# Last turn's last layer in halves, bias rows spread by a product, three x loads first, 25 early sums and three late batches

## The chip, the cores and the metric

The kernel runs on one core of a Trainium2 chip. The metric is the device time of one execution in microseconds (us); lower is better. A run is given as the median of several executions. Beside them one execution was recorded by the hardware profiler; its engines are called PE (matrix products; PEld are its weight loads), DVE (vector), ACT (activation functions and copies), POOL (the general engine) and SP (here it only issues transfers).

## The reference

32 graphs of 512 nodes with 128 features go through four layers, each added to its input after a normalization. `adj` is a 0/1 matrix, symmetric, with ones on its diagonal. Cut to what matters:

```python
# x: (32, 512, 128), adj: (32, 512, 512)
h = relu(layernorm(x))                       # layer 0: masked attention
q, k, v = relu(h @ Wq.T + bq), relu(h @ Wk.T + bk), relu(h @ Wv.T + bv)
x = x + softmax(where(adj, q @ k.T, -inf)) @ v

h = relu(layernorm(x))                       # layer 1: weights made by an LSTM
dyn = conv1d(h[:, -128:, :], conv_w) + conv_b
lw = lstm(dyn)                               # 128 steps, one after the other
x = x + sigmoid(A_norm @ h @ lw)             # A_norm = D^-1/2 (adj + I) D^-1/2

nodes = relu(layernorm(x))                   # layer 2: four layers, each reads earlier ones
for i in range(4):                           # of 128, 128, 256, 384 inputs
    src, dst, own = nodes @ ws + bs, nodes @ wd + bd, nodes @ wn + bn
    new = tanh(concat(l2norm(adj, 2) @ src, own, l2norm(adj, 1).T @ dst) @ wu + bu)
x = x + new

h = relu(layernorm(x))                       # layer 3
y = adj.T @ (h @ W.T) + bias
x = x + prelu(y, a)
```

## The kernel before, in words

**A plan makes the order.** The program is written as a list of operations. Each has an engine (or two to choose from), an estimated duration, a rank, and what it reads and writes. `Plan.run` simulates the engines with these durations and gives out operations in the order in which they could start, the lower rank first. The order found is the order of each engine's queue on the chip, and each queue runs strictly in it. Some constants steer the simulation: `HOLD`, the time by which an operation of other work may still overlap an awaited step of the LSTM; `AHEAD`, `KEEP` and `FETCH`, a model of how many PE instructions have been fetched; `LEAD`, taken off the rank of the operations of the last turn's end.

**The stages.** `pass_1` treats every batch: load x, normalize, transpose, keys, values, the last 128 rows of the attention (`f_pk`, `f_pql`, `f_pv`, `f_sl`, `f_pol`), and the convolution (`f_pd`), whose result goes into `seq`. `fold(i)` multiplies layer 2's weights into two matrices per input, with weights loaded in pass 1 at the positions in `FOLD_AT`. The LSTM then runs 128 steps for all batches together (`f_z` on PE, tanh on ACT, the cell on DVE, a transpose into `seq` on DVE, L1349). Between its steps, `pass_2` does the other 384 rows of the attention (`f_pq`, `f_s`, `f_po`). Of 32 batches the first 24 (`EARLY`) also form layer 1's sums there (`f_pg`) and store them; two (`FIRST`) are kept in memory for the first turns after the LSTM; two (`NEXT`) follow them; the last four (`LATE`) get a rank behind these. Then `rest` does layers 1 to 3, one batch per turn, 32 turns, with neighbouring turns interleaved on PE.

**The start.** Parameters are loaded beside x on ACT's queue by `load_beside`: the attention's weights, the column biases, and row `R_V` of the biases, spread to all 128 partitions by the transfer. Then the table of exp is loaded. The row of the convolution's bias is loaded in the same spread manner on SP's queue (`w_crow`). Ranks of SP put x of the first batch first, then each batch's x and last adjacency columns `f_al` in turn. `warm_up` products on a tile of zeros keep PE busy until data are there: 20 at the start.

**The end.** In the last turn (number 31) each of layer 2's four layers is: `f_py` (a product per 128 nodes with folded weights, onto a bias that ACT or DVE wrote into the bank), split into two parts (`f_y`, L1501 and L1502), eight products with the adjacency into `f_pa` (L1538), a scaling on DVE (L1654), the product with the node's own weights (L1658), and tanh (L1662). After the last one `f_n4T` transposes the result, DVE adds it to x (L1679), `relu_first` normalizes all four tiles of x, with one power on POOL (L1091), and splits them (L1525 on ACT, L1527 on DVE). Products with the adjacency go into two half banks (L1693), are copied to `f_g`, and are multiplied by W (`f_p`, L1706). Then come three steps on each half: DVE adds the positive part (L1709), ACT takes the negative part (L1713), DVE adds it scaled (L1714), and it is stored (L1719). Turns 29 and 30 put off L1713, L1714 and the store until the last turn's split is made; their L1709 comes at once. 16 warm-up products stand in the last turn behind `f_n4T`. At the very end every engine loads a flag that says whether the inputs have the assumed form (L1753), after the stores have been issued, and branches past a general version of the program.

Of the kernel before, what the change touches and what calls it, by code (L numbers as in the profile page):

```python
# [9 lines left out]
AF = mybir.ActivationFunctionType  # L10
# [3 lines left out]
P = 128  # L14
# [507 lines left out]
class Plan:  # L522
# [15 lines left out]
    HOLD = 0.15  # L538
    AHEAD = 264
    FETCH = 4.8  # L540
    KEEP = 32
# [71 lines left out]
    def run(self, tc, queues):  # L613
# [15 lines left out]
        for o in ops:  # L629
            if o.rank >= self.last:  # L630
                k, sub = divmod(o.rank - self.last, 10)
                if sub == 2:
                    apart.add(o)
                soon = self.soon if k < 2 and sub < 2 else 0.0
                first = self.lead if sub == 4 else 0.0
                o.rank = self.last - soon + 12 * k - 9 * max(0, k - 28) + 200.0 - first - (min(behind[o], 60) if sub == 5 else behind[o] + (70 if sub == 2 else 0.0))
# [157 lines left out]
def symmetric(ctx, tc, x, adj, weights, cols, rows, lstm_b, prelu_a, out, fail):  # L794
# [19 lines left out]
    LATE = 4  # L814
    FIRST = [B - LATE - 2 + k for k in range(2)]
    EARLY = range(24)
    NEXT = [len(EARLY), len(EARLY) + 1]
    FOLD_AT = (2, 3, 4, 5)
# [4 lines left out]
    FIRST_GAPS = (2.0, 2.8, 3.0, 3.5)  # L823
    LEAD = 0.0
    Q_AT = 3
    MOVED = range(2, B - 2)
    TURN = 32
    T_STEP = 0.22
    SOON = 9_950.0
    LANDED = 3.3  # L830
# [44 lines left out]
    def t_act(n):  # L875
        return 0.17 + n * 0.0006
# [81 lines left out]
    def load_beside(dst, src, c, gap):  # L958
        return ACT(HEAD, 0.45, lambda: nc.scalar.dma_start(dst, src), [], [c], gap=gap)

    w_att, w_cols = plan.fixed(w), plan.fixed(colb)
    load_beside(w[:, :W_CONV, :], weights[:, :W_CONV, :], w_att, 3.5)
    load_beside(colb, cols, w_cols, 3.0)
    load_beside(brow[:, BR_V, :], rows[R_V].partition_broadcast(P), (biases, BR_V), 3.0)
    ACT(HEAD, 1.5, lambda: nc.scalar.activation(table, neg_half[:, 0, 0:1], AF.Exp))
    w_conv = load(HEAD + 12, 192, w[:, W_CONV:W_IH, :], weights[:, W_CONV:W_IH, :])
    w_crow = load(HEAD + 12, 64, conv_row, rows[R_CONV].partition_broadcast(P))
# [18 lines left out]
    for k in range(20):  # L986
        warm_up(HEAD, 0.43 if k < 8 else 0.216, f"f_warm_{k}")

# [3 lines left out]
    def fill(rank, dst, src, r, c, after):  # L992

        def mark():
            if not c.marked:
                nc.tensor.matmul(c.t, marks[:, :P], marks[:, : c.size], start=True, stop=True)

        def act():
            mark()
            nc.scalar.copy(dst(), src)  # L1000

        def dve():
            mark()
            nc.vector.tensor_copy(dst(), src)
        return plan.op({"ACT": (t_act(c.size), act), "DVE": (t_dve(c.size), dve)}, rank, r, [c], after)
# [158 lines left out]
    def pass_1(b, pos):  # L1164
        R = 10_000 + pos * 10
        xc = new("x", (P, NT, P), f"f_x_{b}")
        n = 2 if pos == 0 else NT
        for at in range(0, NT, n):
            DMA(R, 64 * n, lambda at=at: nc.sync.dma_start(xc.t[:, at : at + n, :], x[b].rearrange("(t p) d -> p t d", p=P)[:, at : at + n, :]), [],
                [(xc, t) for t in range(at, at + n)] if pos == 0 else [xc], gap=FIRST_GAPS[pos] if pos < len(FIRST_GAPS) else 3.5)  # L1170
# [11 lines left out]
        if pos == 0:  # L1182
# [32 lines left out]
        fill(R, lambda: pv.t, bias(BR_V), [(biases, BR_V)], pv, [turned])  # L1215
# [298 lines left out]
    def relu_first(rank, xc, name):  # L1514

        mv = ln_stats(rank, xc, range(NT), name)
        rs = new("rs", (P, NT), f"f_rs_{name}")
        ln_rstd(rank, mv, 0, NT, (lambda: rs.t[:, :], rs), True)
        y = new("xn", (P, NT, P), f"f_yr_{name}")
        parts = new("y", (P, NT, 2, P), f"f_xp_{name}", FR)  # L1520
        for t in range(NT):
            DVE(rank, t_dve(P), lambda t=t: nc.vector.tensor_scalar(y.t[:, t, :], xc.t[:, t, :], mv.t[:, t, 0:1], 0.0, OP.subtract, OP.max),
                [(xc, t), (mv, t)], [(y, t)])
        for t in range(NT):
            ACT(rank, t_act(P) + 0.13, lambda t=t: nc.scalar.activation(parts.t[:, t, 0, :], y.t[:, t, :], AF.Relu, scale=rs.t[:, t : t + 1]),  # L1525
                [(y, t), rs], [(parts, (0, t))])
            DVE(rank, t_dve(P), lambda t=t: nc.vector.scalar_tensor_tensor(  # L1527
                parts.t[:, t, 1, :], y.t[:, t, :], rs.t[:, t : t + 1], f32(parts.t[:, t, 0, :]), OP.mult, OP.subtract),
                [(y, t), rs, (parts, (0, t))], [(parts, (1, t))])
        for finish in put_off:  # L1530
            finish(parts.parts[0, NT - 1][0], parts.parts[1, NT - 1][0])
        return parts
# [19 lines left out]
    def state_of(b, lw):  # L1552

        return nc.sync.dma_start(lw.t.rearrange("t (j f) -> t j f", f=TURN), dh.t.rearrange("(j b) t f -> b t j f", b=B)[b])

    def rest(b, turn, lw_after):
# [83 lines left out]
        for i, nch in enumerate(L2_CHUNKS):  # L1640
            py = bank(f"f_py_{b}_{i}", (P, NT, P), filled=True)
# [24 lines left out]
        if moved:  # L1666
            n4, _ = by_transfer(R, lambda: nodes[4].t, nodes[4], "gs", f"d{b}")
            p4, p4_t = n4, lambda: n4.t
        else:
            p4 = bank(f"f_n4T_{b}", (P, NT, P))  # L1670
            p4_t = lambda: flat(p4.t)

            def back():
                turn_tiles(p4.t, lambda t: nodes[4].t[:, bass.ts(t, P)])
            end4 = PE(R, 4 * T_TR, back, [nodes[4]], [p4])
        if turn == B - 1:
            for k in range(2 * BUFS["mm"]):
                warm_up(R - 4, 0.216, f"f_warm_{k}_{b}", [end4])
        DVE(R, t_dve(N), lambda: nc.vector.scalar_tensor_tensor(flat(xc.t), p4_t(), 0.5, flat(xc.t), OP.add, OP.add),  # L1679
            [p4], [xc])  # L1680
# [7 lines left out]
        for at in range(0, NT, n) if n < NT else ():  # L1688
            cols = slice(at * P, (at + n) * P)
            p3a = bank(f"f_pg3_{b}_{at}", (P, n * P), whole=False)  # L1690
            for k in range(2):
                for j in range(NT):
                    agg3 = PE(R, t_r(n * P), lambda p3a=p3a, cols=cols, k=k, j=j: nc.tensor.matmul(  # L1693
                        p3a.t, hp.t[:, j, k, :], ar.t[:, j, cols], start=(k == 0 and j == 0), stop=(k == 1 and j == NT - 1)),
                        [(hp, (k, j)), ar], [p3a], count=2)
            evict(R, n * P, lambda cols=cols: g3.t[:, cols], lambda p3a=p3a: p3a.t, [p3a], [(g3, at)])
        neg = new("xn", (P, NT, P), f"f_neg_{b}")

        for at in range(0, NT, n):
# [4 lines left out]
            def fc_mm(at=at, p3=p3):  # L1704
# [4 lines left out]
            DVE(R, t_dve(n * P), lambda p3=p3, part=part: nc.vector.scalar_tensor_tensor(  # L1709
                flat(xc.t[:, part, :]), flat(p3.t), 0.0, flat(xc.t[:, part, :]), OP.max, OP.add), [p3], mine)  # L1710

            def finish(turned=(), split=(), at=at, p3=p3, part=part, mine=mine):
                ACT(R, t_act(n * P), lambda: nc.scalar.activation(neg.t[:, part, :], p3.t, AF.Relu, scale=-1.0), [p3], [(neg, at)], after=turned)  # L1713
# [7 lines left out]
            if turn in (B - 3, B - 2):  # L1721
                put_off.append(finish)
            else:
                stored = finish()
            if turn == B - 1:
                late.append(stored)
# [6 lines left out]
    def counted():  # L1733
# [21 lines left out]
        PE(R + 4, 0.1, read, [], [], after=[said] + late)  # L1755
# [105 lines left out]
```

## Time and profile before

| | |
|---|---|
| median of 3 runs | 1277.38 us (1276.59 to 1277.43) |
| the profiled execution | 1275.34 us |
| its span, first to last instruction | 1273.4 us |
| busy: PE, DVE, ACT, POOL | 1255.8 (99%), 985.9 (77%), 837.8 (66%), 400.7 us (31%) |
| weight loads PEld | 970.9 us (76%) |
| moved by transfers | 232.02 MB, mean 182 GB/s |

The span is 1.94 us shorter than the profiled execution's time, and that execution is 2.04 us shorter than the median. A busy PE is not PE at its peak: the ends of products are modelled, so the time from one start to the next says more than the busy share. In the chain of waits a line is: start in us, length in us, what ran; each piece was released by the one above it.

### The profile page before, as it was taken

Reading aid. Unit: us, or ns where it says so; the run is one execution under the profiler, and the core shown is the slowest. Engines: PE = TensorE matmul, PEld = TensorE weight load, DVE = VectorE, ACT = ScalarE, POOL = GpSimd, SP = SyncE. Lnnn points to the kernel's source line nnn. Section 1 sums busy time; section 2 is a strip of 40 time slices with the busy share of each in tenths; the row PEclk is TensorE's granted clock in tenths of the full one; section 3 lists DMA queues with packets and bytes.
Section 4 is the critical chain, followed back from the end, with each engine's and each line's share of the span. In section 5 each row is a group of like instructions: output and inputs, shape, how many; then the busy total and the mean of one; then the engine's idle time right before and its main releaser. Section 6 shows DMA issues by size and latency. Waiting matters only on the chain.

```text
span 1273.4 us, 33089 instructions
## 1 busy us (share of the span) xinstructions
PE 1255.8 (99%) x12074; PEld 970.9 (76%) x12075; DVE 985.9 (77%) x3275; ACT 837.8 (66%) x2102; POOL 400.7 (31%) x734
## 2 busy tenths in 40 slices
PE   9999999999999999999999999999999999999997
PEld 7988876666666767777778787787787877877775
DVE  7899869989899889775677677676776776787755
ACT  4667677778777667774576676666766766675433
POOL 3556533324233135331223233232242232332001
PEclk9999999999999999999999999999999999999999
DMA  8888887778986797876476677777777777482211
GB/s 270 255 274 277 275 270 233 213 226 272 277 259 214 213 251 210 174 175 160 83 178 156 155 173 160 153 174 152 175 154 151 175 157 153 89 174 59 50 33 37
DMA packets 313052, 232.02 MB, mean 182 GB/s; under 512 B 151601, under 2 KB 258481, under 8 KB 312881
## 3 DMA queue, kind: packets, MB, share of 16 engines
q1 hardware_dynamic: 295280, 212.65, 61.5%
q0 software_dynamic: 16896, 16.78, 8.5%
q8 instruction: 97, 1.59, 0.5%
q14 instruction: 75, 0.61, 0.2%
q10 hardware_dynamic: 704, 0.40, 0.1%
HBM read 135.73 MB, written 62.58 MB: 156 GB/s over the span
## 4 chain that ended last, share of the span: by engine, by line
PE 86%; DVE 6%; POOL 2%; ACT 2%; DMA 2%; issue 1%; SPq 0%; ACTq 0%; DVEq 0%
PE f_pa L1538 18%; PE f_py L1647 15%; PE f_pa L1658 15%; PE f_pg L1538 8%; PE f_po L1415 5%; PE f_z L1303 4%; PE f_s L1409 4%; PE f_pol L1251 2%; PE f_pk L1177 2%; PE f_p L1706 2%; PE f_sl L1241 2%; PE f_pv L1219 2%; PE f_pl L1612 2%; PE f_pd L1276 2%; PE f_pq L1399 1%; DVE f_e L1413 1%
## 5 line engine op out<-in xcount | busy, mean ns | idle before, releaser
L1538 PE MATMUL f_pa<-f_ar,f_y 128*128 128x512 f32 x1024 | 298.0, 428 | 0.2 <-ACT f_y L1501 0.2
L1538 PEld LDWEIGHTS f_pa<-f_ar,f_y 128*128 128x128 f32 x1024 | 189.3, 188 | 73.1 <-issue 38.7
L1647 PE MATMUL f_py<-f_wf,f_n 128*128 128x128 f32 x1280 | 173.7, 275 | 0.0
L1647 PEld LDWEIGHTS f_py<-f_wf,f_n 128*128 128x128 f32 x1280 | 165.0, 191 | 10.1 <-issue 2.9
L1662 ACT ACTIVATE f_n<-f_pa,f_bcol 128x512 f32<-128x512 f32 x128 | 88.3, 690 | 101.9 <-PE f_pa L1658 99.0
L1658 PE MATMUL f_pa<-f_n,f_wf 128*128 128x512 f32 x320 | 152.7, 593 | 0.1
L1456 ACT ACTIVATE f_ar<-f_a 128x512 fp32r<-128x512 f32 x224 | 138.7, 622 | 4.1 <-PE f_pg L1538 2.4
L1463 POOL DMA_DIRECT2D f_das<-f_ar x32 | 27.1, 846 | 360.2 <-ACT f_ar L1456 338.1
L1501 ACT CAST f_y<-f_py 128x512 fp32r<-128x512 f32 x128 | 75.3, 589 | 72.1 <-PE f_py L1647 65.5
L1502 DVE TENSOR_TENSOR f_y<-f_py,f_y 128x512 fp32r<-128x512 f32 x128 | 87.7, 687 | 34.9 <-ACT f_y L1501 33.4
L1654 DVE TENSOR_TENSOR f_pa<-f_pa,f_inv 128x512 f32<-128x512 f32 x128 | 86.9, 694 | 28.0 <-PE f_pa L1538 27.9
L1415 PE MATMUL f_po<-f_v,f_e 128*32 128x129 f32 x3072 | 108.0, 273 | 0.4 <-DVE f_e L1413 0.2
L1415 PEld LDWEIGHTS f_po<-f_v,f_e 128*32 128x32 f32 x3072 | 90.9, 110 | 21.1 <-issue 16.6
L1658 PEld LDWEIGHTS f_pa<-f_n,f_wf 128*128 128x128 f32 x320 | 57.9, 190 | 47.0 <-issue 42.6
L1409 PE MATMUL f_s<-f_q,f_k 128*32 128x384 f32 x928 | 92.0, 486 | 0.2 <-issue 0.2
L1303 PE MATMUL f_z<-f_w,f_seq 128*32 128x128 f32 x2040 | 83.4, 276 | 5.2 <-DVE f_seq L1349 2.3
L1303 PEld LDWEIGHTS f_z<-f_w,f_seq 128*32 128x32 f32 x2040 | 53.0, 109 | 45.1 <-ACT f_e L1412 10.0
L1132 DVE COPY f_hl_d<-f_n 128x1024 uint16<-128x1024 uint16 x27 | 18.7, 694 | 88.0 <-ACT f_n L1662 88.0
L1472 DVE SCALAR_TENSOR_TENSOR f_aT<-f_a,f_aT 128x1024 bf16<-128x1024 f32 (+1 forms) x68 | 76.3, 1152 | 0.5 <-DMA f_aT<-f_das 0.5
L1647 PE MATMUL f_py<-f_wf,f_T_c 128*128 128x128 f32 x448 | 72.8, 275 | 0.0
L1538 PE MATMUL f_pg<-f_ar,f_xp_d 128*128 128x512 f32 x248 | 71.9, 413 | 0.0
L1538 PE MATMUL f_pg<-f_ar,f_xp_c 128*128 128x512 f32 x256 | 68.4, 407 | 0.6 <-ACT f_xp_c L1509 0.4
(213 smaller groups left out, 2755.1 us busy)
## 6 DMA issues: line engine op xcount, KB each, us to landing
f_a<-in_adj_dram SPq DMA_DIRECT2D x112, 256.0 KB
f_a<-in_adj_dram SPq DMA_DIRECT2D x28, 1024.0 KB
f_das<-f_ar POOLq DMA_DIRECT2D x32, 512.0 KB, 4.8
f_dkq<-f_kh SPq DMA_DIRECT2D x29, 448.0 KB
f_al<-in_adj_dram SPq DMA_DIRECT2D x32, 256.0 KB
f_inv<-f_ddi SPq DMA_DIRECT2D x32, 256.0 KB
f_x<-in_x_dram SPq DMA_DIRECT2D x31, 256.0 KB
out_dram<-f_x SPq DMA_DIRECT2D x31, 256.0 KB
```

The source lines that it names most:

```text
L1303: nc.tensor.matmul(z.t[part, k, :, :], h, w[:, m : m + 4, part], start=False, stop=True, skip_group_check=True)
L1409: PE(R, t_mm(NR), lambda s=s, j=j: quarters(lambda p: nc.tensor.matmul(s.t[p], keys_of()[:, j * P + p.start : j * P + p.stop], q_of(), sta ...
L1415: PE(R, t_mm(P), lambda e=e, t=t, j=j: quarters(lambda p: nc.tensor.matmul(po.t[p, t, :], e.t[:, t * P + p.start : t * P + p.stop], v.t[:, ...
L1456: ACT(rank, 0.62, lambda t=t: nc.scalar.activation(ar.t[:, t, :], a.t[:, t, :], AF.Square, accum_out=deg.t[:, t : t + 1]), [(a, t)], [(ar, ...
L1472: nc.vector.scalar_tensor_tensor(flat(aT.t[:, n * k : n * (k + 1), :]), flat(a.t[:, n * k : n * (k + 1), :]), 1.0, flat(aT.t[:, n * k : n ...
L1501: ACT(rank, t_act(N), lambda: nc.scalar.copy(parts.t[:, :, 0, :], src.t), [src], [(parts, 0)])
L1502: DVE(rank, t_dve(N), lambda: nc.vector.tensor_sub(parts.t[:, :, 1, :], src.t, f32(parts.t[:, :, 0, :])), [src, (parts, 0)], [(parts, 1)])
L1538: nc.tensor.matmul(pg.t, parts.t[:, j, k, :], ar.t[:, j, :], start=(k == 0 and j == 0), stop=(k == 1 and j == NT - 1))
L1647: nc.tensor.matmul(py.t[:, j, :], nodes[n].t[:, bass.ts(j, P)], wf[:, W_F[i] + c, 0, :], start=False, stop=(c == nch - 1), skip_group_chec ...
L1654: before = DVE(R, t_dve(N), lambda pa=pa: nc.vector.tensor_mul(pa.t, pa.t, inv_row.t), [inv_row], [pa])
L1658: nc.tensor.matmul(pa.t, wf[:, W_F[i] + c, 1, :], nodes[n].t, start=False, stop=(c == nch - 1), skip_group_check=True)
L1662: ACT(R, 0.57, lambda pa=pa, n=n, i=i: nc.scalar.activation(n.t, pa.t, AF.Tanh, bias=bcol[:, i : i + 1]), [pa], [n])
```

## The change

It does the following; parts that only rename are left out.

- The last turn's fourth layer (`BY_HALVES = (3,)`) is written by `layer_by_halves`: banks, splits, products and tanh over 256 columns at a time. `update_by_halves` transposes and adds each half, and `relu_first` has statistics and power for each half.
- In turns 29 and 30 L1709 is put off too; in turn 30 it waits for the last turn's split. L1713 is now ordered behind L1709.
- The last turn's warm-up products are 4 behind the transpose and 3 behind the last product with the adjacency, instead of 16. At the start they are 17 instead of 20.
- The flag is loaded after the copies to `f_g` instead of after the stores, and with a lower rank (R + 3 gets 60 taken off).
- At the start, two bias rows come in one transfer to one partition; a product with ones spreads them, and ACT copies them out. The load order on ACT's queue is column biases, table of exp, weights, rows. SP issues x of three batches before all else. The first batch's fill of `f_pv` is on ACT alone.
- `EARLY` 24 to 25, `LATE` 4 to 3 (so `FIRST` is 27, 28 and `NEXT` 25, 26), `FOLD_AT` one position later, and constants of the plan.

```diff
-    HOLD = 0.15
+    HOLD = 0.18
...
-    FETCH = 4.8
-    KEEP = 32
+    FETCH = 4.5
+    KEEP = 48
...
-                first = self.lead if sub == 4 else 0.0
+                first = self.lead if sub == 4 else 60.0 if sub == 3 else 0.0
...
-    LATE = 4
+    LATE = 3
...
-    EARLY = range(24)
+    EARLY = range(25)
...
-    FOLD_AT = (2, 3, 4, 5)
+    FOLD_AT = (3, 4, 5, 6)
...
-    FIRST_GAPS = (2.0, 2.8, 3.0, 3.5)
-    LEAD = 0.0
+    FIRST_GAPS = (2.0, 3.5, 4.0, 4.0)
+    LEAD = 3.0
...
-    LANDED = 3.3
+    LANDED = 2.8
...
-    load_beside(w[:, :W_CONV, :], weights[:, :W_CONV, :], w_att, 3.5)
     load_beside(colb, cols, w_cols, 3.0)
-    load_beside(brow[:, BR_V, :], rows[R_V].partition_broadcast(P), (biases, BR_V), 3.0)
     ACT(HEAD, 1.5, lambda: nc.scalar.activation(table, neg_half[:, 0, 0:1], AF.Exp))
-    w_conv = load(HEAD + 12, 192, w[:, W_CONV:W_IH, :], weights[:, W_CONV:W_IH, :])
-    w_crow = load(HEAD + 12, 64, conv_row, rows[R_CONV].partition_broadcast(P))
+    load_beside(w[:, :W_CONV, :], weights[:, :W_CONV, :], w_att, 3.0)
+    two_rows = flat(seq[:, : 2 * P // B, :])
+    nc.vector.memset(two_rows, 0.0)
+    w_rows = plan.fixed(two_rows)
+    load_beside(two_rows[0:1], rows[R_V : R_CONV + 1].rearrange("(o r) f -> o (r f)", o=1), w_rows, 2.5)
+    w_conv = load(HEAD + 22, 192, w[:, W_CONV:W_IH, :], weights[:, W_CONV:W_IH, :])
+    w_crow = plan.fixed(conv_row)
...
-    for k in range(20):
+    for k in range(17):
         warm_up(HEAD, 0.43 if k < 8 else 0.216, f"f_warm_{k}")
+
+    spread = bank("f_spread", (P, 2, P), whole=False)
+    PE(HEAD, t_mm(2 * P), lambda: nc.tensor.matmul(flat(spread.t), ones, two_rows, start=True, stop=True), [w_rows], [spread])
+    ACT(HEAD, t_act(P), lambda: nc.scalar.copy(brow[:, BR_V, :], spread.t[:, 0, :]), [spread], [(biases, BR_V)])
+    ACT(HEAD + 11, t_act(P), lambda: nc.scalar.copy(conv_row, spread.t[:, 1, :]), [spread], [w_crow])
...
-            DMA(R, 64 * n, lambda at=at: nc.sync.dma_start(xc.t[:, at : at + n, :], x[b].rearrange("(t p) d -> p t d", p=P)[:, at : at + n, :]), [],
+            DMA(R if pos > 2 else HEAD + pos, 64 * n, lambda at=at: nc.sync.dma_start(xc.t[:, at : at + n, :], x[b].rearrange("(t p) d -> p t d", p=P)[:, at : at + n, :]), [],
...
+    def layer_by_halves(R, b, i, nodes, ar, inv_row, before):
...
+        n = new(f"n{i + 1}" if i < 3 else "gs", (P, N), f"f_n{i + 1}_{b}")
+        nodes.append(n)
+        for at in range(0, NT, HALF):
+            cols = slice(at * P, (at + HALF) * P)
+            pa = bank(f"f_pa_{b}_{i}_{at}", (P, HALF * P), whole=False)
+            for k in range(2):
+                for half in range(0, NT, HALF):
+                    def quarter(pa=pa, cols=cols, k=k, half=half):
+                        for j in range(half, half + HALF):
+                            nc.tensor.matmul(pa.t, parts.t[:, j, k, :], ar.t[:, j, cols], start=(k == 0 and j == 0),
+                                             stop=(k == 1 and j == NT - 1))
+                    PE(R, HALF * t_r(HALF * P), quarter, [(parts, (k, half)), ar], [pa], count=2 * HALF)
+            before = DVE(R, t_dve(HALF * P), lambda pa=pa, cols=cols: nc.vector.tensor_mul(pa.t, pa.t, inv_row.t[:, cols]), [inv_row], [pa])
...
+            PE(R, nch * t_mm(HALF * P), own, [nodes[m] for m in CHUNKS[i]], [pa])
+            ACT(R, t_act(HALF * P) + 0.1, lambda pa=pa, cols=cols: nc.scalar.activation(n.t[:, cols], pa.t, AF.Tanh, bias=bcol[:, i : i + 1]),
+                [pa], [(n, at)])
...
-            for k in range(2 * BUFS["mm"]):
+            for k in range(4 if two else 7):
                 warm_up(R - 4, 0.216, f"f_warm_{k}_{b}", [end4])
...
+            for k in range(3 if at else 0):
+                warm_up(R - 4, 0.216, f"f_warm_{k}_{at}_{b}", [agg3])
...
+                up = DVE(R, t_dve(n * P), lambda: nc.vector.scalar_tensor_tensor(
+                    flat(xc.t[:, part, :]), flat(p3.t), 0.0, flat(xc.t[:, part, :]), OP.max, OP.add), [p3], mine, after=split if turn in WAITING else ())
...
-        PE(R + 4, 0.1, read, [], [], after=[said] + late)
+        PE(R + 3, 0.1, read, [], [], after=[said] + late)
```

## Prediction

> **What bounds the kernel now.** I read the page first, then the chain of waits, then busy time by stretch.
>
> ```profile
> PE 1255.8 (99%) x12074; PEld 970.9 (76%) x12075; DVE 985.9 (77%) x3275; ACT 837.8 (66%) x2102; POOL 400.7 (31%) x734
> PEclk9999999999999999999999999999999999999999
> L1303 PE MATMUL f_z<-f_w,f_seq 128*32 128x128 f32 x2040 | 83.4, 276 | 5.2 <-DVE f_seq L1349 2.3
> ```
>
> PE is the bound nearly everywhere; the change removes no matrix product but warm-ups. So only PE's idle time can be won: at the start, between LSTM steps, at the end. The chain at the start:
>
> ```profile
> 0.74 3.25 DMA f_w<-in_weights_dram
> 4.00 0.34 SPq L955
> 4.39 6.28 DMA f_x<-in_x_dram
> 10.70 0.48 DVE f_st_a L1081 x2
> 11.18 0.39 DVE f_kh L1180
> 11.71 1.14 PE f_sl L1241 x8
> ```
>
> SP issues the third batch's x only at 4.39; it lands at 10.67. DVE, in order, stands before its statistics, and behind them stands the first batch's key copy (L1180), for which PE waits until 11.71. The chain at the end:
>
> ```profile
> 1250.07 2.58 PE f_pa L1658 x6
> ...
> 1253.57 0.90 PE f_p L1706 x8
> ...
> 1254.57 0.70 DVE f_x L1709
> ...
> 1255.92 0.75 DVE f_x L1714
> 1256.67 0.61 DVE f_x L1679
> ...
> 1258.76 0.59 PE f_warm L984 x2
> 1259.35 0.89 PE f_p L1706 x8
> 1260.24 0.86 PE f_warm L984 x4
> ...
> 1263.45 1.09 PE f_warm L984 x5
> ```
>
> The last turn's result is ready at 1252.64, but its update (L1679) starts at 1256.6: its transposes stand behind other turns' products, and DVE behind turn 28's L1709 and L1714. Later PE runs warm-ups while inputs are there.
>
> ```profile
> L1753 PEldq TENSOR_LOAD <-fail x1: 488/488/488, 1265.9 to 1265.9; - x1
> L1753 SPq TENSOR_LOAD <-fail x1: 485/485/485, 1266.8 to 1266.8; - x1
> 1267.00:1268.00 1.00, 0.00 (x0) 0.00 (x0) 0.00 (x0) 0.00 (x0) 0.00 (x0) 1.00 0.68 177
> 1268.00:1269.00 1.00, 0.00 (x0) 0.00 (x0) 0.00 (x0) 0.00 (x0) 0.00 (x0) 0.54 0.40 106
> ```
>
> The flag is loaded behind the stores; nothing computes from 1266.83 to 1273.4. The last two lines (stretch, length, five engines, PE clock, transfers) show the clock falling.
>
> **The end: -1.9 us.** Halving adds no PE work: 8 products of 512 columns take 1.85 us, and 128x256 products run at 0.118 (10 in 1.18 us). It adds fixed cost: a 256-column DVE step is 0.42-0.43 us against 0.69, so three split steps cost 0.45 more; on ACT about 0.4; two POOL powers of about 0.69 (the first batch's pair: 1.38) against 1.07 add 0.3, on a POOL queue that holds nothing else after 1259 but its flag load. In return half 0 runs 1.3 us ahead (half of 2.58), and half 1 has less behind it: tanh 0.45 for 0.69, transposes 0.22 for 0.44, update 0.42 for 0.69, two statistics 0.43 for 0.87, power 0.7 for 1.07, two ACT splits instead of four (1.28): about 2 us less latency.
>
> Two floors say how much can show. PE after 1252.64: products of turns 28 to 30 (two f_pg halves 1.86, one f_pg of 1.85, three f_p at 0.89, transposes and flag sum 0.5) and the last turn's own 16 (1.87) are 8.8 us, to 1261.4, where before they ended at 1263.45: -2.0. DVE is busy 10.55 of the 12.37 us from 1254.5 to 1266.87, so without idle it ends 1.8 earlier, 3.0 if half 0's 1.2 us move into the idle DVE of 1250-1254 (1.98 of 4 us busy), less the 0.45. Putting turn 30's L1709 (0.69) behind the split lets L1527 start at 1260.3 instead of 1260.96; it then lies in DVE's wait of 1.1 us before the last f_p. Its cover is that wait; if DVE is not idle there, it costs 0.69. L1713 behind L1709 is nothing new: ACT already waited 1.7 us for it. Warm-ups were 3.0 us of the chain above; the seven left cost at most 7x0.216 = 1.5. I take -1.9, the lower end of both floors; bounds -3.0, and +0.5 if the held banks of turns 29 and 30 (two of eight) and the small banks of the halves make them wait for one another.
>
> The clock: by the row it is full to about 1268.1 (0.54 is 0.5 and 0.08 us of full), 1.8 us after the last product (1265.92+0.38). The Trainium skill (TensorE: Matmul & The Clock Gate, Part 1: The HAM clock gate) says that a window of 3.4 us without work halves it; that speaks against cutting warm-ups. If it fell, 16 f_pg and 8 f_p would take 2.8 us more. Neither row nor rule gives that: without 9 warm-ups the longest hole is the copy to f_g, under 1 us. I count 0.
>
> **The flag: -0.4 us.** Its load leaves the path on SP (0.485 us) and ACT (0.48). PE, with the lower rank, may load it ahead of the second half's f_p: +0.49 in the worst case; DVE and ACT load it in their wait for f_p (1.1 and 1.7 us). What remains is larger: SP's load ends at 1267.3, its next instruction comes at 1271.8. From the trace alone an earlier load might move all of this forward. The Trainium skill (Runtime: NRT & Kernel Launch, Instruction fetch mechanics) says that fetch runs ahead only in sequence and that a taken branch to a page not held waits for its transfer. Then the 4.5 us start at the branch, still behind the stores; by the rule -0.5, by the other reading up to -1.5 (how much earlier PE loads it). I follow the rule; bounds -0.5 and +0.5.
>
> **The start: -1.2 us.** PE's products from 7.24 to 14.02 are 4.1 us (f_xt, f_pk, f_pql, f_pv, f_sl, f_xt, f_wT at 0.44, 0.86, 0.22, 0.89, 0.89, 0.44, 0.33), so 2.7 us are idle; from 14.02 it is full. Issuing x of the third batch before 2.5 instead of 4.39 takes away DVE's 1.17 us wait and PE's 0.9 us hole: -0.9. SP's f_al slips by some 0.5 us; its first user (L1246) is at 13.58. The two spread rows (64 KB each; 0.34 us of SP's issue, 0.48 of ACT's) go, for one row transfer of 1 KB on ACT. The convolution weights slip a batch on SP; their user starts at 21.45. FOLD_AT moves 0.33 us of transposes out of a hole: later work, same sum. ACT's queue: the weights go behind the table load (1.28) and its activation (0.2), so are issued at about 2.7 instead of 0.74; with the same 3.25 us they land at 6.0, before f_pk at 8.30. Without them beside it x of the first batch may land earlier (192 KB at 267 GB/s: 0.7 us), and 17 warm-ups end 0.65 earlier; the spread product (two passes of 256 columns, 0.43) takes most of that back: -0.3. Its danger: it is in PE's queue ahead of the first transposes; rows issued at 3.2 land at about 6.4, warm-ups end at 6.5. If rows come later, all of PE waits, one for one. ACT has two copies (0.37 each) and the fill (0.59) more, in its idle 8.53-10.11. Bounds -2.7 and +0.7.
>
> **The LSTM's stage: -0.9 us.** 187.9 to 493.0 is 127 steps of 2.40 us. A stretch such as 445-465 holds 212 f_po, 72 f_s, 16 f_pq, 132 f_z and 8 f_pg, at their spacing (0.0275, 0.081, 0.081, 0.027, 0.23) 18.3 of 20 us; so over the stage some 20 us of PE are lulls and changes of tile form. The 25th early batch brings one f_pg (2.04 with its changes) into the stage and takes 1.85 out of PE-bound time: -1.85 if a lull takes it, +0.2 if not; I take half. It also brings DVE about 3.5 us (L1101, L1510, L1479, half an L915) where DVE is busy 273.1 of 308.2, and ACT's squares 4x0.62; 256 KB more stored and fetched, and 1 MB of adjacency again later, beside PE-bound turns at 150-175 GB/s, where earlier stretches carried 280. LATE changes order: at 493 only 168 f_po, under two batches, were left anyway: 0. HOLD, KEEP, FETCH, LANDED change when filler is let in; no row shows it. Bounds: -3 (a seventh of the lulls) and +3.8 (0.03 x 127), value 0, the nearest row being that PE waits only 2.3 us for L1349 in all.
>
> **Sum.** -1.9 - 0.4 - 1.2 - 0.9 = -4.4. The profiled execution, 1275.34 us (span 1273.4 and 1.94 around it), would become 1270.9. It lies 2.04 below the median of the runs; the same change on the median gives 1273.0.
>
> **Rivals.** *More from the stage.* Filler constants and the early batch win 4 us of lulls: 1277.4-3.5-4 = 1269.9. For it: 20 us are there, and 465-485 holds a POOL chain of 6 us. Against: DVE at 89%. *Gains don't show.* PE at the start is held by the spread product (0), the end gives 0.9 because turn 30's own chain (f_g at 1258.3, f_p at 1259.2) ends last: 1276.5. For it: turn 30 was on the chain at 1259.35. Or it doesn't do what it says: the plan, not ranks, sets where half 0 stands, and it may queue right before half 1. *Slower.* HOLD 0.18 lets filler overlap each awaited step by 0.03 us more; on two engines that is 0.06x127 = 7.6 us later LSTM end. Where PE fills this, it costs nothing; where filler waits for data it is lost: 1277.4-3.5+7.6 = 1281.5. It decides from about 0.03 us per step (2.43 us), unless less work is left behind the LSTM. Against: filler remained at 493.
>
> **How the numbers follow.** The likeliest case has 0.55 (own range 1270.8 to 1274.8), more from the stage 0.16, gains don't show 0.18, slower 0.11. A measurement can tell 0.2%, 2.55 us, from no change; so faster 0.71, same 0.18, slower 0.11. The range goes down to 1267.5 (most of the first rival, with the start's bound) and up to 1278.0, beyond which only the slower case lies.
>
> **What would show it.** Right: DVE's first wait for f_x after 5 us gone; PE from about 13 us full; the last f_pg by 1262 on this clock, i.e. 2 us closer behind L1658; TENSOR_LOAD on SP before the last store; still 4 to 5 us from branch to SP's next instruction; L1349 from first to last within 305 +-3 us. Wrong: a PE hole before f_xt, clock under 1.00 before the last f_p, or an LSTM span changed by more than 4 us.

## The result and the profile after

| | before | after |
|---|---|---|
| median of 6 runs each | 1277.41 us (1276.59 to 1279.67) | 1272.21 us (1270.56 to 1273.86) |
| ratio, 95% interval | | 0.9963 [0.9953, 0.9974] |
| profiled execution, its span | 1275.34, 1273.4 us | 1272.32, 1270.4 us |

The kernel became faster by 4.7 us (interval 3.3 to 6.0); the forecast was 1273.0. The two profiled executions differ by 3.0 us only, since that of before lay 2.07 us below its median and that of after 0.11 above. So the traces can be asked where 3.0 us went, and not more.

Five marks cut the span (us; starts, except where an end is named). They are read in every kernel below.

| mark | before | after | stretch before it changed by |
|---|---|---|---|
| first product `f_z` of the LSTM | 185.14 | 184.11 | -1.0 |
| first transpose of a step (L1349; after: L1361) | 187.9 | 188.2 | +1.3 |
| last such transpose | 493.0 | 498.2 | +5.0 |
| end of the last own product (L1658; after: L1609) | 1252.64 | 1253.62 | -4.3 |
| end of the last DVE step | 1266.83 | 1265.56 | -2.25 |
| end of the span | 1273.4 | 1270.4 | -1.7 |

**The page of after**, the three lines that were shown of before:

```profile
PE 1251.3 (98%) x12078; PEld 970.2 (76%) x12078; DVE 974.8 (77%) x3267; ACT 835.6 (66%) x2126; POOL 389.6 (31%) x737
PEclk9999999999999999999999999999999999999999
...
L1315 PE MATMUL f_z<-f_w,f_seq 128*32 128x128 f32 x2040 | 83.2, 276 | 7.3 <-DVE f_seq L1361 5.0
```

PE is still the bound at a full clock. In the third line, the idle time of PE before an LSTM product grew from 5.2 to 7.3 us, with 5.0 of it waiting for the step's transpose (before: 2.3).

**The start**, in the chain of waits of after (start us, length us, what):

```profile
1.23 3.34 DMA f_x<-in_x_dram
...
8.28 1.01 POOL f_rs_a L1103
9.30 0.22 POOL f_rs_a L1102
...
9.59 1.08 POOL f_rs_a L1103
...
11.47 0.70 DVE f_kh L915
...
12.21 1.13 PE f_pk L1189 x2
```

No transfer of x stands in the chain after 4.57 us; before, one of 6.28 us ended at 10.67. From 12.21 the chain is PE without a break to 20 us (before: from 14.02). What is late next is POOL: its powers lead to the second batch's key copy, for which PE still waits 0.9 us.

**The end**, the same view:

```profile
1251.04 2.59 PE f_pa L1609 x12
1253.62 0.89 PE f_p L1791 x8
1254.52 0.44 PE f_n4T L1624 x4
1254.95 2.81 PE f_pg L1555 x12
...
1258.77 0.67 PE f_warm L991 x3
1259.43 0.89 PE f_p L1791 x8
1260.33 2.00 PE f_pg L1776 x16
1262.32 0.88 PE f_warm L991 x4
1263.20 0.97 PE f_p L1791 x8
```

The DVE pieces between PE's are gone: PE goes through from 1251 to 1264.17, with 1.55 us of warm-ups among it. Half 0's tanh does come 1.3 us before half 1's (1252.37 and 1253.66), but the lead is not used: in PE's queue its transposes stand behind `f_p`, and all four go in one piece (x4, third line). What moved is DVE's order (DVE in after, in order of time, cut):

```profile
1253.39 0.69 DVE L1522 SCALAR_TENSOR_TENSOR f_xp_d<-f_xn_d,f_xp_d 128x512 fp32r<-128x512 f32 x1 [1.25 <-ACT f_xp_d L1521]
1254.55 0.69 DVE L1795 SCALAR_TENSOR_TENSOR f_x<-f_p,f_x 128x512 f32<-128x512 f32 x1 [0.47 <-PE f_p L1791]
1255.16 0.74 DVE L1627 SCALAR_TENSOR_TENSOR f_x<-f_n4T,f_x 128x256 f32<-128x256 f32 x2
...
1256.95 0.72 DVE L1798 SCALAR_TENSOR_TENSOR f_x<-f_neg,f_minus_alpha,f_x 128x512 f32<-128x512 f32 x1
```

The update (L1627) starts 1.54 us after the own product's end (before 3.95). Another turn's split (L1522) now runs ahead of turn 28's L1795 (before behind it, at 1255.17), and turn 28's L1798 comes behind the update. The last split (L1544) ends 6.9 us after the own product (before 9.4).

**The flag and the branch** (instruction, count, shortest/median/longest ns, first and last start):

```profile
L1835 SPq TENSOR_LOAD <-fail x1: 477/477/477, 1262.3 to 1262.3; - x1
L1835 PEldq TENSOR_LOAD <-fail x1: 736/736/736, 1262.7 to 1262.7; - x1
L1883 SPq COMPARE_BRANCH  x1: 53/53/53, 1265.5 to 1265.5; - x1
L1930 SPq DRAIN  x3: 7/7/13, 1269.5 to 1269.8; - x3
```

and of before, the branch and the DRAIN:

```profile
L1801 SPq COMPARE_BRANCH  x1: 53/53/53, 1267.4 to 1267.4; - x1
L1848 SPq DRAIN  x3: 7/7/13, 1272.5 to 1272.8; - x3
```

In after the loads lie before the last store (1265.6). SP branches 0.07 us before the last DVE step ends, where before it was 0.56 behind it. From the branch to SP's first DRAIN, near the program's end, 4.0 us pass (before 5.1). SP's waits at the branch's line (us in all, times, longest; the view names no releaser but SP itself), before and after:

```profile
SPq L1801 <- SPq L1801: 3.9, 3, 2.9
```

```profile
SPq L1883 <- SPq L1883: 2.6, 1, 2.6
```

The longest one is that for SP's first instruction behind the branch, which starts 2.97 us after it in before and 2.67 in after. Up to the DRAIN follow twenty waits for semaphores (counters by which engines and transfers say that they are done), the first of them that instruction. They take 1.36 us in after, where the last stores have landed (1267.66 and 1268.09) before SP comes to them. In before they take 2.16, since two of them wait for the landing of the last two stores (1270.96 and 1271.34). So of the 1.7 us in the last row of the marks 0.6 are the branch's place, 0.3 the first instruction behind it, and 0.8 the stores.

The clock stayed full behind the last product:

```profile
1266.00:1267.00 1.00, 0.00 (x0) 0.00 (x0) 0.00 (x0) 0.00 (x0) 0.00 (x0) 1.00 0.91 262
1267.00:1268.00 1.00, 0.00 (x0) 0.00 (x0) 0.00 (x0) 0.00 (x0) 0.00 (x0) 0.67 0.20 48
```

**The stage.** PE, in order of time, at the LSTM's first step, of before and then of after:

```profile
185.14 1.27 PE L1303 MATMUL f_z<-f_w,f_seq 128*32 128x128 f32 x40
```

```profile
184.11 0.40 PE L1315 MATMUL f_z<-f_w,f_seq 128*32 128x128 f32 x8
184.33 0.83 PE L1421 MATMUL f_s<-f_q,f_kh 128*32 128x384 f32 x8
184.97 0.40 PE L1427 MATMUL f_po<-f_v,f_e 128*32 128x129 f32 x8
185.19 0.83 PE L1421 MATMUL f_s<-f_q,f_kh 128*32 128x384 f32 x8
185.84 1.06 PE L1315 MATMUL f_z<-f_w,f_seq 128*32 128x128 f32 x32
```

Before, the first step's 40 products stood in a row. Now attention filler stands between the first 8 and the other 32: the gain of the start is lost by the first transpose. The whole stage by busy time (stretch, length, then busy PE, PEld, DVE, ACT, POOL, PE clock, transfers), before and after:

```profile
187.90:493.00 305.10, 299.38 (x6305) 209.43 (x6301) 272.50 (x1130) 227.78 (x811) 97.27 (x178) 1.00 0.81 242
```

```profile
187.90:498.30 310.40, 301.58 (x6319) 210.88 (x6312) 271.35 (x1126) 232.91 (x819) 93.53 (x175) 1.00 0.79 237
```

PE idles 8.8 us in after and 5.7 in before (length less the first number), and does 2.2 us more work.

### The profile page after: what moved, and what is told of

Read it like the earlier page. It is cut to its first block, busy times and chain, and to the rows that moved or that the text cites. A ratio compares the mean times of both kernels' runs of the same rounds, so it can differ in the third digit from the quotient of the medians.

```text
span 1270.4 us, 33137 instructions
## 1 busy us (share of the span) xinstructions
PE 1251.3 (98%) x12078; PEld 970.2 (76%) x12078; DVE 974.8 (77%) x3267; ACT 835.6 (66%) x2126; POOL 389.6 (31%) x737
## 4 chain that ended last, share of the span: by engine, by line
PE 83%; DVE 7%; DMA 4%; ACT 3%; POOL 2%; issue 1%; SPq 0%; DVEq 0%; ACTq 0%
PE f_pa L1555 17%; PE f_py L1726 15%; PE f_pa L1737 15%; PE f_pg L1555 7%; PE f_s L1421 4%; PE f_po L1427 3%; PE f_z L1315 3%; PE f_pol L1263 2%; PE f_pk L1189 2%; PE f_p L1791 2%; PE f_sl L1253 2%; PE f_pv L1231 2%; PE f_pl L1688 2%; PE f_pd L1288 2%; DMA f_dx<-f_x 1%
## 5 line engine op out<-in xcount | busy, mean ns | idle before, releaser
L1555 PEld LDWEIGHTS f_pa<-f_ar,f_y 128*128 128x128 f32 x1016 | 187.9, 188 | 72.9 <-issue 38.3
L1424 ACT ACTIVATE f_e<-f_s 128x384 f32<-128x384 f32 x128 | 60.7, 484 | 13.1 <-PE f_pg L1555 7.7
```

Source lines behind the costliest of these rows:

```text
L1555: nc.tensor.matmul(pg.t, parts.t[:, j, k, :], ar.t[:, j, :], start=(k == 0 and j == 0), stop=(k == 1 and j == NT - 1))
```

## The experiments

All were timed against the kernel before, 5 rounds (ratio with 95% interval). The marks of their profiled executions, in us:

| kernel | ratio | first `f_z` | first, last transpose | last own product starts | last DVE step starts | span |
|---|---|---|---|---|---|---|
| before | 1 | 185.1 | 187.9, 493.0 | 1252.0 | 1266.3 | 1273.4 |
| after | 0.9963 [0.9953, 0.9974] | 184.1 | 188.2, 498.2 | 1253.2 | 1265.1 | 1270.4 |
| b_flag | 0.9998 [0.9988, 1.0008] | 185.4 | 188.1, 495.0 | 1254.3 | 1269.0 | 1274.6 |
| b_tail | 0.9992 [0.9981, 1.0002] | 184.7 | 187.5, 493.0 | 1252.6 | 1264.6 | 1271.3 |
| b_head | 1.0042 [1.0028, 1.0055] | 184.0 | 191.6, 497.0 | 1254.3 | 1268.6 | 1276.4 |
| b_stage | 1.0058 [1.0045, 1.0072] | 186.2 | 189.0, 494.4 | 1258.5 | 1272.8 | 1279.4 |
| b_tailflag | 0.9976 [0.9966, 0.9986] | 185.1 | 187.8, 496.4 | 1256.0 | 1267.8 | 1273.4 |
| a_nostage | 0.9989 [0.9979, 0.9998] | 183.4 | 191.0, 499.6 | 1256.6 | 1268.5 | 1274.2 |
| a_oldconst | 1.0359 [1.0334, 1.0384] | 183.3 | 190.9, 500.5 | 1304.7 | 1316.5 | 1322.2 |
| a_oldearly | 1.0031 [1.0020, 1.0043] | 184.5 | 188.6, 498.5 | 1259.5 | 1271.3 | 1276.9 |
| a_oldhead | 1.0028 [1.0015, 1.0040] | 187.0 | 189.8, 501.1 | 1266.6 | 1278.5 | 1284.4 |
| a_first | 1.0388 [1.0363, 1.0414] | 184.3 | 187.2, 494.2 | 1307.9 | 1319.7 | 1325.4 |
| a_nostage_first | 0.9977 [0.9966, 0.9988] | 183.6 | 186.1, 495.6 | 1254.1 | 1265.9 | 1271.6 |
| a_lateflag | 0.9985 [0.9976, 0.9995] | 185.1 | 189.2, 500.0 | 1254.9 | 1266.8 | 1273.2 |

How far one execution may be trusted: b_flag has before's order up to the last turns, b_tail and b_tailflag have it through the LSTM's stage, and a_lateflag has after's up to the last turns. Before and these three differ by up to 0.7 us at the first `f_z` and 3.4 at the last transpose, before and b_flag by 2.3 at the last own product; after and a_lateflag differ by 1.0, 1.8 and 1.6. So differences of 2 to 3 us in these columns tell nothing. The profiled executions of a_oldearly and a_oldhead lie 3.4 us below and 4.4 above the medians of their kernels, the other trials' within 2.1. But the tail's stretch (start of the last own product to start of the last DVE step) is 14.3 in each old tail (b_flag 14.7) and 11.8 to 11.9 in each new one.

**One part alone, on the kernel before.** *b_flag*, the flag only:

```diff
-                first = self.lead if sub == 4 else 0.0
+                first = self.lead if sub == 4 else 60.0 if sub == 3 else 0.0
...
-            evict(R, n * P, lambda cols=cols: g3.t[:, cols], lambda p3a=p3a: p3a.t, [p3a], [(g3, at)])
+            late.append(evict(R, n * P, lambda cols=cols: g3.t[:, cols], lambda p3a=p3a: p3a.t, [p3a], [(g3, at)]))
...
-        PE(R + 4, 0.1, read, [], [], after=[said] + late)
+        PE(R + 3, 0.1, read, [], [], after=[said] + late)
```

> Kernel before with the flag's earlier load alone. Theory A (the branch's fetch starts at the branch; only the load of 0.48 us leaves the path): 0.4 to 0.5 us less, from the last store's issue to the end 6.1 us become 5.6. Theory B (with the loads away the five branches come further apart, and their fetches no longer wait for one another): 1.5 to 1.8 us less, from the last store's issue to the end about 4.4 us, as in the changed kernel. Everything up to the last turn as before.

Measured: 1276.49 us against 1276.99. SP branches 0.4 us before the last DVE step ends (before 0.56 behind it), which is 1.0 us earlier, and reaches its DRAIN 4.7 us after it. Of the 1.0 us some 0.6 are left, for the tail's stretch is 14.7, 0.4 longer: DVE now does the second half's L1709 behind the first half's L1714. The timing can't tell it from no change; a gain of up to 1.5 us lies within its interval.

*b_tail*, the last turn's halves, the put-off of turns 29 and 30, `LEAD` and the warm-ups of the end (cut to the constants; the code is that of the change):

```diff
-    LEAD = 0.0
+    LEAD = 3.0
+    BY_HALVES = (3,)
+    PUT_OFF = (B - 3, B - 2)
+    WAITING = (B - 2,)
```

> Kernel before with the last turn's halves, the put-off steps, LEAD 3 and 7 warm-ups in the tail alone; the flag as before. The prediction: 1.9 us less. By the two traces, from the last own product's end (L1658) to the last DVE step, 14.2 us become 11.9: 2.3 us less. Rival (turn 30's chain ends last): 0.9 us less.

Measured: 1275.36 us. By the ratio it is 1.0 us faster, and anything from 2.4 faster to 0.3 slower lies within the interval, so the timing alone tells neither 1.9 from 0.9 nor either from no change. The tail's stretch is 11.9, 2.4 shorter than before. Behind it SP's branch comes 1.44 after the last DVE step's end (before 0.56). The load is the same 0.48 us; what is longer is the issue of SP's last store, 1.21 us where ACT issues its own beside it (at 1265.07), against 0.37 in before:

```profile
1264.67 1.21 SPq L1794 DMA_DIRECT2D out_dram<-f_x  x1
```

*b_head*, the start with its loads, spread product, `FOLD_AT` and `FIRST_GAPS` (cut; the loads and the product are those of the change):

```diff
-    FOLD_AT = (2, 3, 4, 5)
+    FOLD_AT = (3, 4, 5, 6)
...
-    for k in range(20):
+    for k in range(17):
         warm_up(HEAD, 0.43 if k < 8 else 0.216, f"f_warm_{k}")
```

> Kernel before with the start alone (x of three batches first, rows by a product, order on ACT's queue, folds a position later, 17 warm-ups). The prediction: 1.2 us less, all of it before the first LSTM product (185.1 us before, 184.1 in the changed kernel). Rival: the 1.0 us gained there is given back in the LSTM's stage, whose order is laid anew, and the time is the same within 0.5 us.

Measured: 1280.2 us, slower. The first `f_z` comes 1.1 earlier, the first transpose 3.7 later: 8 products at 184.00, the other 32 only at 189.20, with filler between. So the loss shows first in the order of the LSTM's first step, not in the start.

*b_stage*, `EARLY`, `LATE` and the four constants:

```diff
-    HOLD = 0.15
+    HOLD = 0.18
...
-    FETCH = 4.8
-    KEEP = 32
+    FETCH = 4.5
+    KEEP = 48
...
-    LATE = 4
+    LATE = 3
...
-    EARLY = range(24)
+    EARLY = range(25)
...
-    LANDED = 3.3
+    LANDED = 2.8
```

> Kernel before with EARLY 25, LATE 3, HOLD, KEEP, FETCH and LANDED of the changed kernel alone. The prediction: 0.9 us less. Rival (the two traces, in which the LSTM ended 5.2 us later and only 4.2 us came back behind it): about 1 to 2 us more, LSTM steps of 2.44 instead of 2.40 us. If neither, within 0.5 us: a matter of the one execution that was traced.

Measured: 1282.83 us, slower. The step is 2.405 us (before 2.402), so `HOLD` did not lengthen it here. The loss lies behind the LSTM: from its end to the last own product 764.2 us, before 759.1; PE is busy 18.87 and 18.61 of 20 us in 500 to 540, before 19.44 and 20.00.

Added up, the four parts would make 1.009 (product of the ratios), 11.5 us slower; together they are 4.7 faster. So they do not add, and the next runs take one part out of the whole.

**One part back, from the changed kernel.** *a_nostage*, *a_oldconst* and *a_oldearly* put back all six constants, the four, or the two (shown are the two; the four are those of b_stage the other way round):

```diff
-    LATE = 3
+    LATE = 4
...
-    EARLY = range(25)
+    EARLY = range(24)
```

> Changed kernel with the stage's constants of before (EARLY 24, LATE 4, HOLD, KEEP, FETCH, LANDED). Theory additive (each part keeps the worth it had alone, where the stage cost 0.58% and the start 0.42%): the time of before times 1.0042 less the tail, about 1280 us. Theory joint (every edit lays the order of the whole middle anew, and what counts is how the new order fits): no sum holds; the pass before the LSTM and the tail keep their gains of 1.0 and 2.3 us in the trace, and the middle, from the first LSTM product to the last own product (L1658), is what moves, by up to 5 us either way against the changed kernel's 1069.

> Changed kernel with HOLD, KEEP, FETCH and LANDED of before (EARLY 25 and LATE 3 kept). Theory constants (they were set for this order, and they carry the gain): 4 us or more above the changed kernel's 1272.2. Theory joint: the middle moves by up to 5 us with no rule for its sign. The prediction's sum (value 0): within 1 us of the changed kernel.

> Changed kernel with EARLY 24 and LATE 4 (constants of the plan kept as changed). The prediction (25th early batch worth 0.9): 0.9 us above the changed kernel. Theory joint: the middle moves by up to 5 us, seen in the step of the LSTM (2.44 us changed) and in holes of PE in the 40 us behind it.

Measured: 1276.26, 1323.83 and 1282.36 us, against 1278.43 for before beside them. With the old constants (a_nostage, a_oldconst, and b_head) 7.6 us pass from the first `f_z` to the first transpose, with the new ones and the new start 4.1 (after, a_oldearly), with the old start 2.7 to 2.8 under either. So start and constants act on each other, through the order of the LSTM's first step. In a_oldconst the stage then starves at its end: stretches of after, then of a_oldconst:

```profile
460.00:480.00 20.00, 19.69 (x432) 13.44 (x424) 17.89 (x79) 11.08 (x39) 6.55 (x14) 1.00 0.60 147
480.00:500.00 20.00, 18.92 (x300) 14.05 (x299) 18.30 (x75) 15.04 (x52) 8.29 (x17) 1.00 0.79 231
```

```profile
460.00:480.00 20.00, 8.68 (x132) 5.15 (x133) 6.90 (x34) 5.51 (x26) 0.00 (x0) 0.50 0.03 8
480.00:500.00 20.00, 12.26 (x140) 6.31 (x144) 6.40 (x31) 5.95 (x27) 0.00 (x0) 0.59 0.03 7
```

PE is half idle, transfers carry 8 and 7 GB/s instead of 147 and 231, and the clock falls to 0.50 and 0.59. SP's queue in that time:

```profile
460.15 40.67 SPq L1364 DMA_DIRECT2D f_dh<-f_h  x5
504.70 4.11 SPq L1455 DMA_DIRECT2D f_dgT<-f_x  x3
508.91 0.88 SPq L1399 DMA_DIRECT2D f_a<-in_adj_dram  x2
```

Five stores of LSTM outputs follow one another, each of four steps and so some 10 us apart, with no fetch of adjacency between them: nothing for the filler is on its way until 508.9. This order is the plan's. Why its simulation left the queue so was not settled.

*a_oldhead*, the changed kernel with the start of before:

> Changed kernel with the start of before. Additive: start alone cost 0.42%, so without it 5 us less, 1267. Prediction: 1.2 us more, 1273.4. Joint: first LSTM product about 1 us later than the changed kernel's 184.1, and the middle off by up to 5 us, as in the kernel with the stage alone, where PE had holes of 4 us behind the LSTM while adjacency was awaited.

Measured: 1281.81 us. The first `f_z` is at 187.0, the first transpose 2.8 later, and the last own product 765.5 behind the LSTM's end (after: 755.0). The ratios put it 8.3 us behind after, far more than the 1 to 1.5 us of the new start (the traces say more still, since this execution lay 4.4 above its median); the rest is the order's doing.

**The first step's order by itself.** *a_first* and *a_nostage_first*: the changed kernel, and a_nostage, with

```diff
-        PE(2_000, MANY * T_STEP, lambda z=z: first(z), [], [z], after=conv_ops, tiled=True, count=64)
+        PE(-1, MANY * T_STEP, lambda z=z: first(z), [], [z], after=conv_ops, tiled=True, count=32)
```

> The changed kernel, with the first products of the LSTM (32 of a first step's 40 products of f_z) given rank -1 and a count of 32 instead of rank 2000 and 64, so that the plan puts them ahead of attention filler. Theory: the new start lost 1.3 us to filler in the midst of the first LSTM step (first f_z at 184.1, first transpose 4.1 later, before the change 2.8). Then first transpose 2.7 to 3.0 us after the first f_z, at about 187; LSTM end about 1.3 earlier. The end in time is less sure, since the rest of the stage is laid out anew: about 1271 (0.995) if only the hole goes. Rival: the stage's later order decides alone; the first transpose comes earlier but the last own product is anywhere within 5 us of 1253.

> The changed kernel with EARLY 24, LATE 4 and the old plan constants, and the first LSTM products at rank -1, count 32. Without the rank this kernel had its first f_z at 183.4 and its first transpose at 191.0, and took 1276.3. Theory: the 7.6 us from the first product to the first transpose were the plan's, made by its model of fetched instructions; with the rank they become 2.7 to 3.0, and the LSTM ends 4 to 5 us earlier. If that carries to the end, about 1271.5 (0.995). Rival: the LSTM's end is not what PE waits for, and the earlier end only turns into more PE-bound work behind it: 1275 to 1277.

Measured: both have the gap closed, with 2.9 and 2.5 us from the first to the first transpose. a_nostage_first took 1275.11, 0.9977 against 0.9989 for a_nostage: of 4.9 us at the first transpose 4.0 are left at the LSTM's end, 2.6 at the last own product, and 1.5 by the ratios (intervals overlap, and 2 to 3 us in the marks can be chance). a_first took 1327.47: in it too five stores stand alone in SP's queue, from 454.98 for 39.52 us. That the plan's place for the first products made the gap of 1.3 us is shown, but mending it laid out the rest anew, in a_first far worse.

**The end by itself.** *b_tailflag*, the two diffs of b_tail and b_flag on the kernel before:

> The kernel before with the end by halves, the put-off, the warm-ups of the end and the early flag; the start, EARLY, LATE and the plan's constants as before. Theory: tail and flag are local and add, -2.4 from last own product to last DVE step and -1.4 behind it, with nothing lost in the middle: about 1273.6 (0.997), as fast as the whole change to within 1.5 us. Rival: the parts don't add, because each edit lays out the stage anew: then the first two marks stay (own to last DVE 12.0, end 5.3 to 5.9), and the LSTM's end to the last own product leaves 759 by more than 2 us.

Measured: 1274.48 us, 3.1 less than before (interval 1.8 to 4.3). The tail's stretch is 11.8, the end behind the last DVE step's end 5.1 (before 6.58). The end carries about two thirds of the gain; that it is less than the whole change is not resolved, since the intervals overlap.

*a_lateflag*, the changed kernel with the flag behind the stores again:

```diff
-        PE(R + 3, 0.1, read, [], [], after=[said] + late)
+        PE(R + 4, 0.1, read, [], [], after=[said] + late)
```

> The changed kernel with the flag loaded behind the stores again, at its old rank. The order differs from the changed kernel's only in the last turns. Theory A (the forecast's): only the load leaves the path, so from the last DVE step to the span's end 4.84 becomes about 5.3, and the time 0.5 longer. Theory B: the late load also makes the branch dearer, as the kernel before showed (6.57 from the last DVE step to the end, 4.5 from SP's load to its next instruction): 6.5, and about 1.7 us longer, 1274. With B, PE's and SP's time from the load to their next instruction is 4 us or more.

Measured: 1274.97 us, 0.9985. SP, in the same view as above:

```profile
L1837 SPq TENSOR_LOAD <-fail x1: 484/484/484, 1267.7 to 1267.7; - x1
L1885 SPq COMPARE_BRANCH  x1: 53/53/53, 1268.2 to 1268.2; - x1
L1932 SPq DRAIN  x3: 7/7/13, 1272.3 to 1272.6; - x3
```

The last DVE step ends at 1267.27 and the span 5.9 us later: between A's 5.3 and B's 6.5. The lines tell them apart. SP branches 0.96 behind the last DVE step's end (after: 0.07 before it), and from the branch to the DRAIN it takes 4.1 us, where after takes 4.0. (B's mark of 4 us or more was badly set: both kernels meet it.) So the branch is no dearer for a late load, which is A's mechanism. But the branch comes 1.0 us later, twice A's size: 0.5 is the load, and most of the rest is again SP's last store, whose issue took 0.73 us beside ACT's (after: 0.37):

```profile
1266.90 0.73 SPq L1803 DMA_DIRECT2D out_dram<-f_x  x1
```

By the ratios the kernel is 2.8 us (1.0 to 4.6, from the two intervals) behind after; what this is beyond the 1.1 us behind the last DVE step stays open.

None of these kernels beat the changed one.

## Why the prediction was right, point by point

The time fell within 0.8 us of the forecast. Its working holds less well: in the traces the sum is -3.0 instead of -4.4, with the terms of the start and the end about right, 1.3 us more than forecast behind the last DVE step, and 2.9 us less in the stage. The medians are nearer only because before's profiled execution was a short one. So that the number came so close is partly luck.

- **The end, -1.9: right.** -2.25 in this pair from end to end, and 2.4 to 2.9 less from start to start in every kernel with the new tail than in one with the old. The PE floor held: from the last own product to the last `f_pg` 8.70 us, before 10.81, the 2.0 forecast. But half 0's 1.3 us of running ahead, a part of the reasoning, were lost at the transposes, close to what the second rival doubted, and the two powers on POOL took 1.19 and 0.69 us instead of 0.69 each. The gain came without them; the chain puts it down to the order on DVE and to fewer warm-ups (1.55 us of them are left on the chain, as bounded; before 3.0). No run takes halves, put-off steps, `LEAD` and warm-ups apart, so each one's share is not shown. The held banks made nothing wait in the chain.
- **The clock, 0: right.** It is full to 1267.34 (0.67 in the last stretch is 0.34 us of full and 0.66 at half), 3.2 us after the last product; before it was 1.8. No product of after met the low clock. The rule as the forecast put it, a window of 3.4 us without work (the Trainium skill, TensorE: Matmul & The Clock Gate, Part 1), doesn't give these figures: over the 14 kernels the clock fell 1.8 to 4.8 us behind the last product. Nor does it take a stretch without work (last section).
- **The flag, -0.4: about right for what it counted, from a misread line.** The load's 0.48 us, with the gap behind it 0.55, left SP's path: SP's branch moved by 0.6 us against the last DVE step in this pair, and b_flag nets 0.6. (Where a late flag cost more, 1.0 and 1.5 us, SP's last store took longer to issue as well.) But SP's next instruction behind the branch came at 1270.4 in before, 3.0 us after it, and not at 1271.8; what lay between were waits for semaphores. The rule that was followed (the Trainium skill, Runtime: NRT & Kernel Launch, Instruction fetch mechanics: fetch runs ahead only in sequence) fits: that first instruction starts 2.6 to 3.2 us after the branch in the five kernels with a late flag, whose load stands right ahead of the branch, and 2.7 to 3.3 in the nine with an early one, loaded about 3 us ahead. The other 1.1 us of the pair's 1.7 were in no term: 0.3 lie within this spread, and 0.8 are the wait for the last stores. b_head and b_stage, with before's end, wait 0 and 0.2 us there, so most of it may belong to before's one execution.
- **The start, -1.2: right up to the LSTM.** -1.0 in this pair; the mean over kernels is 185.6 with the old start (six) and 184.0 with the new one (eight). The spread product did not hold PE: the first product of `f_xt` is at 6.87, before at 7.45. Three steps inside were wrong. The working counted PE's idle time from 7.24, where the last warm-up starts, and so 2.7 us instead of 2.5. The weights did not wait for the table load (below). And that filler would stand within the LSTM's first step was not foreseen; it took the 1.0 us back before the first transpose.
- **The LSTM's stage, -0.9: not borne out.** From the first `f_z` to the end of the last own product it is +2.0 in this pair (1067.5 to 1069.5 us). But b_flag, with before's order, takes 1069.5 too, and a_lateflag, with after's, 1070.2: a loss isn't shown either. What failed is the constants' value of 0, with bounds -3 to +3.8. With `EARLY` and `LATE` they cost 7.4 us on the kernel before; on the changed one, putting back all six costs 3.3 us and the four alone 51. Over all twelve trial kernels this middle stretch, to the start of the last own product, takes 1067.9 to 1079.6 us in ten and 1121 to 1124 in two (before 1066.9). The half of -1.85 for the early batch can't be told apart in this. The LSTM's span changed by 5.0 us, over the 4 that were to prove the forecast wrong; over executions it is 305.1 to 308.6 us in four of before's order and 310.1 and 310.9 in two of after's.
- **The rivals.** *Slower* set its point at 2.43 us per step; 2.441 was measured, and the LSTM ended 5.3 us later. `HOLD` isn't shown to be the cause (b_stage has it and takes 2.405, b_tailflag has the old one and takes 2.430), and 4.3 of the 5.3 us came back behind the LSTM, where PE was filled, which the text gave as the condition for no cost. *More from the stage* has nothing for it: PE's idle time there rose from 5.7 to 8.8 us. Most of the 4.7 us is the end with its flag (b_tailflag, 3.1); which part won the remaining 1.6, within the intervals, stays open.

## What to carry to other kernels

Where a planner writes the order, an edit has a local worth, which repeats in every kernel (tail 2.4 us, start 1.5, flag 0.6), and a price or gain by laying out everything else anew, which doesn't: here +1 to +13 us over before's one execution in ten kernels, of which 2 can be chance, and +54 and +57 in two. So cut the span by marks, count a part by its own stretch, and hold back a forecast's range for the rest. A constant of such a planner is not worth 0 because no row shows it, and two parts that lose alone may not lose together.

## What was not expected of the hardware

- A load of the activation table did not hold up ACT's issue of transfers. ACT's queue in after, in order of time:

```profile
1.22 1.28 ACT L967 ACT_TABLE_LOAD   x1 [1.22 <-PEq L1924]
1.32 0.38 ACTq L963 DMA_DIRECT2D f_w<-in_weights_dram  x1
1.75 0.56 ACTq L963 DMA_DIRECT2D f_seq<-in_rows_dram  x1
```

  The weights and the rows are issued at 1.32 and 1.75, within the 1.28 us of the load; the forecast had put them behind it, at 2.7 and 3.2.
- One execution of the same order can differ from another by 2 to 3 us at the end of a stage of 300 us or more (493.0 to 496.4 in four), so a single trace of each kernel can't settle a change of 0.2% in the middle.
- The clock fell in the midst of work. In a_oldhead PE had a hole of 1.8 us and was busy for 1.57 of 3.40 us; the next 3.4 us ran at half clock (stretches as above):

```profile
603.10:606.50 3.40, 1.57 (x8) 1.26 (x8) 2.71 (x7) 0.34 (x1) 0.00 (x0) 1.00 0.77 170
606.50:609.90 3.40, 3.40 (x9) 2.31 (x8) 2.30 (x5) 0.00 (x0) 0.00 (x0) 0.50 0.97 303
```

- Behind the same branch POOL, which branches 5 to 8 us ahead of SP, starts its next instruction 2.5 to 2.8 us later in every kernel, and SP 2.6 to 3.3. The 3.9 to 5.1 us to SP's DRAIN hold its twenty waits for semaphores besides, so they are no measure of the branch.
